# Late shared-FFN pieces inside the last sigmoid, their final add on VectorE as a step of its own, and idle matrix products in attention's last group

## The chip, the core and the metric

The kernel runs on one core of a Trainium2 chip. A core has five engines, each with a queue of its own that it works off in order: TensorE (PE; its weight loads are shown as PEld), VectorE (DVE), ScalarE (ACT), GpSimd (POOL) and SyncE (SP, which here only issues DMAs). Engines wait for one another through semaphores. The metric is the device time of one execution in microseconds (us); of several runs the median counts.

## What is computed

An adaptive-norm transformer block on 8 sequences of 512 rows of 256 values, all in f32: latent attention with 16 heads, then a mixture of 16 experts with an expert-choice router (each expert takes the 512 rows with its highest scores) and a shared FFN for all rows. Cut to what matters:

```python
h = _layernorm(x) * (1 + ca) + sa
x = x + ga * attention(h)                      # causal, 16 heads
h = _layernorm(x) * (1 + cb) + sb
# routed experts
scores = sigmoid(h @ gate_w.T)                 # 4096 x 16
topk_score, topk_ids = top_k(scores.T, 512)    # rows per expert
xin = h[topk_ids]
eo = (silu(xin @ gw.T + gb_e) * (xin @ up_w.T + up_b)) @ down_w.T + down_b
out = zeros_like(h).at[topk_ids].add(eo * topk_score)
# shared FFN, all rows
shared = (silu(h @ sh_gate_w.T) * (h @ sh_up_w.T)) @ sh_down_w.T
x = x + gb * (out + shared)
```

## The kernel before

**Attention.** It runs in 32 steps, `steps[n]`, of four heads each; step n belongs to sequence b = n // 4 and group g = n % 4. In the loop at L781 step n does three things side by side: the maxima of the next step (`scores` L569 on PE, `maxima` L575 on DVE), its own exponentials (`scores_t` L598 on PE, `exps` L609 on ACT, a mask on POOL at L613), and the last step's sums over the values (`context` L628 on PE). `fold` (L590, four transposes, then a product on DVE) opens a step, and eight slots follow. Between them, `fill(k)` runs the pieces that `plan(n)` (L662) has put into slot k: norms, projections, the residual of the sequence before. A piece with a cost is moved to a later slot by `laid_out` when PE has no room; a piece with cost 0.0 stays in its slot. In step 31, the last, there is no next step: no `scores` and no `maxima`.

**Shared FFN.** `Shared(b, early)` (L264) does one sequence. Its 24 units are, for each of four blocks f: two gate products and two up products of 512 columns (L276), with Silu on ACT and the product `mid` on DVE (L312); then eight down units of two products of 256 columns (L321). After four down units `put` (L334) multiplies the two finished row tiles by `gb` on DVE (L336), adds x on POOL (L338) and writes the rows to `out` on SP (L339). Sequences 0 and 1 are "early": `plan` takes their units into attention's steps, twice `SHARE[b][g]` at a time, but always whole groups. Sequences 2 to 7, 144 units, go to the queue `late` (L814) and are taken in pairs by `work()` (L816) as filler for PE wherever the rest of the program leaves it idle.

What DVE has to do after a late unit is not issued at once: it is put on the list `later`, and `flush()` (L260) issues all of it, last in first out. `flush()` is called when the next up unit, the next down unit of a new tile or a new sequence begins, and once per bit of the search (L892).

**From attention to the experts.** After step 31 come the `tail` (L823: the last sequence's residual, norm, transposes and router scores, with a pair of units behind each piece), `sigmoid` for the last two sequences (L840; a generator in four parts, about 16 DVE instructions on 128 x 128 values, then two DMAs of the scores), and a transposition of all scores (L872). Then a binary search over 30 bits finds each expert's threshold (L887): per bit DVE counts (L884), PE sums over the sequences (`cnt`, L891), DVE forms `drop` (L894) and `cand` (L896), and one pair of late units goes to PE. Places are then numbered (`gt`, `eq`, `run`, L903 to L943; `pplace` L928), one-hot tables (L962) and index products (L984) give the row numbers `idx` (L995), and four indirect DMAs on POOL gather the first expert's rows (L1002). What is left in `late` runs behind that (L1154), and then the rows are transposed into `xT` (L1014, L1015) and the expert loop begins.

The order is written out by hand: each engine does its instructions in the order in which the program issues them.

## Time and profile before

| what | value |
|---|---|
| median of 3 runs | 1443.43 us (1439.97 to 1443.79) |
| the profiled execution, its own time | 1438.41 us |
| its span, first to last instruction | 1436.7 us |
| PE busy | 1379.9 us, 96% of the span |
| DVE busy | 906.9 us, 63% |
| POOL busy | 561.7 us, 39% |
| ACT busy | 475.9 us, 33% |
| mean granted TensorE clock | 0.970 |
| POOL's adds of x to the shared rows (L338) | 16 of 1398 ns on average |
| DVE's products with gb (L336) | 16 of 688 ns |

The page gives busy time by engine and, for 40 equal slices of the span (35.9 us each), the busy share in tenths; PEclk is the TensorE clock that was granted, in tenths of full speed. A timeline row has start, length, engine, line, operation, names and shapes, how many instructions were merged (x), and in brackets how long the engine stood idle before it and what ended the wait. An f32 product appears as two PE records. A line of the view by stage has a window, its length, and for each engine the busy us and the number of instructions. The chain of work that ended last could be followed back only through the last DMA (2 us), so it says nothing about the middle of the program.

## The change

Four edits, in the same file:

1. `SHARE` for the last sequence becomes (2, 2, 2, 0). Before, step 28 took four units of sequence 1, step 29 eight; now steps 28, 29 and 30 take four each, so that the second group of four down units moves from step 29 to step 30, with its `put`.
2. `put` becomes a generator of two parts: the multiply; then the add of x and the write to `out`. For late sequences the add runs on VectorE instead of GpSimd. The two parts are two entries of `later`, which becomes a queue, first in first out. `flush(n=2)` issues at most two entries; in the search it is `flush(1)`, one entry per bit.
3. The loop over the last sigmoid's four parts calls `work()` after each part. Eight late units thereby run between the parts instead of behind the first gather, and all late units between move forward by eight places. In the order of instructions the sigmoid's first part is followed on VectorE by a multiply and an add of a `put`, the third part by another such pair, and on SP two writes to `out` and one load of `gb` are ahead of the writes of the scores.
4. In step 31 each of the slots 1 to 8 ends with a product of `ident` and 256 columns of `causal`, whose result nobody reads. It goes to one of the three PSUM banks `s`, which the maxima use in the other steps.

```diff
-SHARE = [(0, 0, 0, 0), *[(0, 1, 1, 1)] * 6, (2, 3, 3, 4)]
+SHARE = [(0, 0, 0, 0), *[(0, 1, 1, 1)] * 6, (2, 2, 2, 0)]
...
-    later = []
-
-    def flush():
-        while later:
-            later.pop()()
+    later = deque()
+
+    def flush(n=2):
+        for _ in range(min(n, len(later))):
+            later.popleft()()
...
             if ii == 1 and h == 1:
+                put = self.put(self.py, i2)
                 if self.early:
-                    self.put(self.py, i2)
+                    next(put)
+                    next(put)
                 else:
-                    later.append(lambda py=self.py: self.put(py, i2))
+                    later.append(lambda: next(put))
+                    later.append(lambda: next(put))
 
         def put(self, py, i2):
             ysb = fp.tile([P, 2, D], F32, name="ysb", tag="ysb", bufs=2)
             nc.vector.tensor_tensor(ysb, py, self.gb.unsqueeze(1).to_broadcast([P, 2, D]), ALU.mult)
+            yield
             n = self.b * TT + 2 * i2
-            nc.gpsimd.tensor_tensor(ysb, ysb, x_all[:, n : n + 2, :], ALU.add)
+            eng = nc.gpsimd if self.early else nc.vector
+            eng.tensor_tensor(ysb, ysb, x_all[:, n : n + 2, :], ALU.add)
             nc.sync.dma_start(out_v[:, n : n + 2, :], ysb)
+            yield
...
+    def keep_warm():
+        n = T // 2
+        nc.tensor.matmul(bank_s("warm")[:, 0:n], lhsT=ident, rhs=causal[:, T - n : T], start=True, stop=True)
...
+        if n + 1 == len(steps):
+            for k in range(1, SLOTS):
+                add(k, 0.0, keep_warm)
...
     for _ in sigmoid(B - 2, 2):
-        pass
+        work()
     flush()
...
-            flush()
+            flush(1)
```

## What was predicted

> **What bounds the kernel now.** I read the slices of the page first, then busy time by stage, then the order of instructions in the stages that the change touches.

> ```profile
> PE   8999999999999999997989999999999999999996
> PEclk8899999999999999798999999999999999999998
> ```

> TensorE is busy nearly everywhere; the holes and the lowered clock lie in slices 17 to 22, between the last attention group and the first expert. That is where all the edits are. The experts behind it (773 us to the end) have PE full at clock 1.0 and are not touched: what is won before them comes off the end. The same stretch cut at the clock's own edges (columns: window, length, then busy us and count of PE, PEld, DVE, ACT, POOL, then granted clock, DMA share, GB/s):

> ```profile
> 582.70:589.50 6.80, 6.72 (x36) 4.40 (x40) 2.96 (x14) 2.75 (x7) 1.31 (x3) 0.50 0.00 0
> 596.35:610.00 13.65, 12.94 (x64) 7.50 (x65) 0.23 (x1) 3.62 (x12) 7.64 (x14) 0.50 0.16 44
> 654.97:660.16 5.19, 0.01 (x2) 0.03 (x1) 4.78 (x14) 0.00 (x0) 0.51 (x1) 0.77 0.30 103
> 660.16:668.03 7.87, 6.36 (x18) 5.07 (x19) 2.97 (x11) 0.59 (x1) 1.26 (x1) 0.50 0.63 187
> 668.03:731.03 63.00, 57.84 (x205) 33.09 (x204) 43.44 (x126) 5.97 (x10) 6.31 (x5) 1.00 0.32 116
> 731.03:753.40 22.37, 20.60 (x101) 12.47 (x99) 18.95 (x31) 1.79 (x3) 4.59 (x2) 1.00 0.05 17
> 753.40:771.70 18.30, 17.45 (x62) 10.53 (x58) 4.39 (x8) 1.79 (x3) 5.36 (x5) 1.00 0.31 90
> ```

> See: two stretches at half clock around attention's last group; PE empty for 5.19 us under the sigmoid (DVE 4.78 busy), then half clock for 7.9 us; 5.2 us of holes in the search; PE full of shared pieces in the last row, after the first gather is issued. Two bits of the search, the first with a `mid` product between count and drop, the second with a `put`:

> ```profile
> 682.69 0.28 PE L891 MATMUL cnt<-part,same 128*128 128x1 f32 x2
> 682.96 0.69 DVE L312 TENSOR_TENSOR mid<-pu,sg 128x512 f32<-128x512 f32 x1 [0.76 <-PE pu L276]
> 684.75 0.38 PE L891 MATMUL cnt<-part,same 128*128 128x1 f32 x2
> ...
> 690.92 0.28 PE L891 MATMUL cnt<-part,same 128*128 128x1 f32 x2
> 691.17 0.69 DVE L336 TENSOR_TENSOR ysb<-py,gb 128x512 f32<-128x512 f32 x1 [0.75 <-issue]
> 691.95 1.26 POOL L338 TENSOR_TENSOR ysb<-ysb,x_all 128x512 f32<-128x512 f32 x1 [20.38 <-DVE drop L894]
> 691.96 1.26 DVE L896 SCALAR_TENSOR_TENSOR cand<-drop,cand 128x1 int32<-128x1 int32 x1
> 694.07 0.38 PE L891 MATMUL cnt<-part,same 128*128 128x1 f32 x2 [1.04 <-DVE mask L884]
> ```

> A bit with a mid takes 2.06 us and PE does not wait. In the bit with a put, POOL's add starts 10 ns ahead of the tiny `cand` step, which then lasts 1.26 us (0.16 elsewhere), and PE waits 1.04.

> **The change, part by part.** Times are against the profiled execution: 1438.41 us, of which 1436.7 are span. That execution is 5.0 us below the median of the three timed runs (1443.43), so the saving is taken off the median.

> *Early pieces (SHARE).* Walking the plan, step 29 keeps one group of four down units, and the other goes to step 30; nothing is left over or dropped. A group is 8 products; 16 of them (32 records) took 7.07 us at 763.78, so 3.5 us of PE. Step 29 lasted 19.4 us (fold to fold, 550.8 to 570.1); step 16, which has the full-size PE work that step 29 will have, lasted 17.3: −2.2. Step 30 lasted 16.2 and its load becomes that of steps 14, 22, 26 (17.5, 17.5, 17.8): +1.4. The put that comes along (DVE 0.69, POOL 1.26, an out write on SP) ends at the fold, where DVE is free and waits 2.40 us for pmx; POOL's next piece is 4 us off. Its write stands on SP before `ga`, first read at 607. Net −0.8. Besides, full-size products now lie in step 30's last slots, before 582.7.

> *Idle products.* Eight, ident with 256 columns, one per slot of step 31: nearest row L321, 0.44 us each, 3.5 in all. They are ahead of the next `st_ps` pair on PE's queue. PE waits there for ACT by 0.39 and 0.57 in two of the first four slots, so about 0.6 of the first four is seen, and the others lie in slots that are counted below. What they buy is the clock. [...] in the window before 596.35 no PE gap exceeded 0.57 us, yet the clock fell. [...] In the 3.41 us windows of this trace, I summed columns streamed, weighted by rows times columns of the array in use. From 60 us to the last expert the clock fell after windows of 0.13 to 0.38 and stayed up after those above 0.4 (and two of 0.36 and 0.37). The one at 592.9 has 0.31, the next two 0.17 and 0.19. One idle product adds 0.43/3.41 = 0.13, about two fall in each window: 0.5. The down group adds 0.25 to 0.5 to the window at 579.3 (0.25). So both half-clock stretches should go:
> - 586.3 to 590.0 (fold, `po`): first `st_ps` 1.6 earlier.
> - slots 4 to 7, 596.6 to 604.5, 7.9 us: at full clock with the idle products about 5.5 (pz 0.93 for 1.89, the pairs 0.43 and 0.21 us): −2.4.
> - `po` of the last group: 4.4 at half clock, 2.2 at full: −2.2; first shared product −0.5.
> - visible idle products +0.6.
> Sum −6.1. Bounds: if the clock does not rise, +3; if all are hidden, −7.

> *Pieces between the sigmoid's parts.* Eight late units, in four pairs: two pairs of down (1.97 each) and a gate and an up pair (1.96 each), 7.9 us, fill the hole of 5.2. The DVE chain grows: two puts of 0.69 multiply and 0.69 add go between its parts, some 2.5 us with the overlap of neighbours (0.60 from start to start). Scores ready about 662.5 instead of 660.0, PE done with the up pair at 662.8, the first count at 664.2 instead of 661.95: +2.3. ACT's Silu is 0.6 in its idle time. On SP, two out writes and a `gb` load (0.4 each) pass ahead of score rows and weights; the weights landed by about 690, used at 773. The cold stretch 660.2 to 668.0 goes: the first three bits took 9.7 us where three take 6.2: −3.5 (this includes one put stall of 1.0). Should the 2.3 us of thin PE work around the transposes of the scores fall into one clock window, 1.7 come back.

> *Add on DVE, one piece per bit.* In the search, four more puts of before cost 1.04 to 1.09 each: −4.2. Now the multiply runs between count and drop, as a mid does (no slack left there: 682.69 to 684.75 is just PE's period). The add is put out by the next down or gate, so it stands between `cand` and the next count. Nearest row: back-to-back DVE products, 0.60 apart. Four times +0.6 = +2.4; the bit behind has nothing to flush and cannot give it back. Bounds 0 to 0.69 each. Who waits is count, then PE's `cnt`, then PE's filler. The adds on DVE work beside no POOL work in the search.

> *Behind the search.* All positions move on by eight units. DVE from the last counts to idx: inserted are two puts (1.2, and 0.5 beyond the wait for `pplace`) and a mid (0.6), 2.3; gone are a mid and two multiplies, 1.8, and the stretch of `at_j` and `num` beside POOL (three pieces of 0.72 to 0.77 us, 0.32 on average elsewhere), 1.25. From `pplace` PE has six pairs of 1.72 us and becomes last: idx about 0.7 earlier. Then PE's remaining list:

> ```profile
> 754.95 1.24 POOL L1002 DMA_INDIRECT rows<-rows_d,idx  x1 [2.77 <-DVE mid L312]
> 759.01 0.95 POOL L1002 DMA_INDIRECT rows<-rows_d,idx  x1 [0.30 <-issue]
> 763.78 7.07 PE L321 MATMUL py<-shd,mid 128*128 128x256 f32 x32
> 771.74 1.06 PE L1014 MATMUL pxt<-ident,rows 128*128 128x128 f32 x8 [0.89 <-issue]
> ```

> Ten units behind the gather's issue instead of eighteen; from pi on, PE has a gate pair, an up pair and the 7.07 us of down: 10.5 us. The last gather lands about 3.7 us after 759.0, 9.3 after pi. So the transposes start some 7.7 us earlier counted from the last counts, with 1.7 us of cover left: the gather is late next. Half a microsecond less is waited for POOL's add before xT.

> **Sum.** −0.8 −6.1 +2.3 −3.5 −4.2 +2.4 −7.7 = −17.6; with the smaller end at xT **−18**. The profiled execution would be 1420, the median **1425**.

> **Rivals.**
> 1. All three work: 1425, own range 1420 to 1431, chance 0.66.
> 2. The clock stays low in the last group (for it: [...] that my weighting is fitted; against it: 0.31 to 0.5 crosses the bound by far). The eight products then cost about 0.85 each, half of it seen, and the 6.1 become +3: 1434. Chance 0.13.
> 3. The gather is no longer covered, by 1 to 4 us, or a clock window is lost at the search's start: for it the cover of only 1.7 us; against it DVE and POOL are emptier there. 1428. Chance 0.14.
> 4. The change moves the hole only (DVE's chain from scores to idx being the true bound, so that the eight units were free where they stood). Against it: PE full in the last row above. Within 0.3%, 1443. Chance 0.04.
> 5. Slower: eight units less behind the gather, and PE stands until it lands. It costs landing minus 10.5 us after pi; to outweigh the 18 the gather must land 28.5 us after pi, three times the 9.3 of the trace. Past that, say at 35, 1449. Nothing in the page supports it. Chance 0.03.

> **The numbers.** Rivals 1 to 3 lie between 1420 and 1435; medians of one kernel differ by some microseconds (the three runs spread over 3.8), hence 1414 to 1436. A change of 0.3%, 4.3 us, is what can be told from none. Faster 0.93 (1 to 3), same 0.04, slower 0.03.

> **What would show it.** Clock 1.0 from 560 to 600 us and through the sigmoid; PE holes there under 2 us; no `cand` step over 0.2 us in the search; PE waits of about 0.6, not 1.04, in four bits; six pairs between pplace and pi; transposes of the first expert directly after the last multiply. The prediction is wrong if the clock row shows 0.5 in the last group, or if PE waits for a gather.

## The result, and the profile after

| | before | after |
|---|---|---|
| median of 4 runs on the same chip | 1441.7 us (1438.53 to 1443.79) | 1420.07 us (1419.21 to 1428.17) |
| ratio | | 0.9864, 95% interval 0.9822 to 0.9906 |
| profiled execution, its span | 1438.41, 1436.7 | 1419.94, 1417.8 |
| mean granted TensorE clock | 0.970 | 0.980 |

The changed kernel is faster, by 21.6 us (1.4%) in the medians and by 18.5 in the profiled executions; the interval of the ratio ends below 1. The slices of its page, busy share and clock of TensorE:

```profile
PE   8999999999999999999999999999999999999996
PEclk8899999999999999999999999999999999999998
```

The dent in slices 17 to 22 is gone from both rows. Line numbers have moved with the edits: `cnt` is L904 now, `cand` L909, the count L897, the two parts of `put` L339 and L343, the gather L1015, the transposes of the gathered rows L1027. The same stretch cut by stage, in the view shown before (window, length, busy us and count of PE, PEld, DVE, ACT, POOL, then granted clock, DMA share, GB/s). The stages are: the last group from its first `st_ps` to the first shared product behind it; from the scores to the first count; from the count of `gt`, the first one behind the search, to the gather's issue; from there to the transposes.

```profile
588.05:604.17 16.12, 16.12 (x120) 8.74 (x116) 0.91 (x3) 6.64 (x17) 9.17 (x17) 1.00 0.09 17
647.92:658.62 10.70, 9.30 (x36) 6.21 (x35) 9.26 (x23) 1.18 (x2) 2.13 (x3) 1.00 0.34 108
...
721.38:744.53 23.15, 21.87 (x104) 13.45 (x103) 19.87 (x36) 1.79 (x3) 0.00 (x1) 1.00 0.09 29
744.53:754.40 9.87, 9.04 (x37) 6.70 (x37) 2.83 (x5) 0.60 (x1) 4.08 (x4) 1.00 0.49 138
```

The clock is 1.00 in every row. TensorE fills the last group without a hole; under the sigmoid it works 9.30 of 10.70 us; and behind the gather's issue there are 9.87 us left where there were 16.8 (754.95 to 771.74 in the trace of before). A bit of the search with a `put`, in the timeline of the changed kernel:

```profile
675.75 0.28 PE L904 MATMUL cnt<-part,same 128*128 128x1 f32 x2
...
675.95 0.69 DVE L339 TENSOR_TENSOR ysb<-py,gb 128x512 f32<-128x512 f32 x1 [0.69 <-PE py L321]
...
676.82 0.68 DVE L343 TENSOR_TENSOR ysb<-ysb,x_all 128x512 f32<-128x512 f32 x1
...
678.23 0.38 PE L904 MATMUL cnt<-part,same 128*128 128x1 f32 x2 [0.36 <-DVE mask L897]
```

The add now lies on DVE ahead of the next count (L897, in the last row's bracket), and PE waits 0.36 us for that count instead of 1.04. And the end of the stretch:

```profile
744.53 1.24 POOL L1015 DMA_INDIRECT rows<-rows_d,idx  x1 [94.32 <-DVE mid L312]
...
746.50 7.07 PE L321 MATMUL py<-shd,mid 128*128 128x256 f32 x32
...
748.57 0.94 POOL L1015 DMA_INDIRECT rows<-rows_d,idx  x1 [0.30 <-issue]
...
754.40 1.06 PE L1027 MATMUL pxt<-ident,rows 128*128 128x128 f32 x8 [0.83 <-issue]
```

The transposes follow directly on the last down products and on the last multiply of the shared FFN; nothing waits for the gather, whose last rows landed at 752.4, 2.0 us ahead of the transposes.

Where the time came from, stage by stage (us, start to start, from the two traces; "predicted" is the term on record; the search runs from the first count on DVE to the last `cnt` on PE):

| stage | before | after | difference | predicted |
|---|---|---|---|---|
| step 28, fold to fold | 19.54 | 19.54 | 0 | 0 |
| step 29 | 19.38 | 16.52 | −2.86 | −2.2 |
| step 30 | 16.17 | 17.21 | +1.04 | +1.4 |
| fold 31 to its first `st_ps` | 3.71 | 2.17 | −1.54 | −1.6 |
| slots 0 to 3 | 6.57 | 7.61 | +1.04 | +0.6 |
| slots 4 to 7 | 7.92 | 6.22 | −1.70 | −2.4 |
| `po`, to the first shared product | 4.42 | 2.29 | −2.13 | −2.2 |
| to the scores | 44.26 | 43.75 | −0.51 | −0.5 |
| scores to the first count | 8.75 | 10.70 | +1.95 | +2.3 |
| first count to the last | 68.41 | 62.09 | −6.32 | −5.3 |
| last count to `xT` | 42.67 | 34.43 | −8.24 | −8.1 |
| `xT` to the first expert's Silu | 6.07 | 4.38 | −1.69 | none |
| experts, to the end | 657.60 | 658.32 | +0.72 | 0 |
| sum from fold 28 on | 905.47 | 885.23 | −20.24 | −18 |

In the row for before, slots 3 and 4 are parted at slot 4's second product (596.59), which waits for ACT; its first had started at 595.16. Parted at the first product, as in the row for after, the two rows are 5.14 and 9.35 before, 7.61 and 6.22 after. Their sum is the same either way, 14.49 and 13.83; only the sum should be read as a gain.

What lies ahead of fold 28 is the same program in both kernels, yet its length is not the same: 531.2 us before and 532.6 after, and 529.7 to 538.4 over all profiled executions of this study. It goes with the time at half clock in that stretch: 41.0 us in the five executions of up to 531.2, 58.0 in the two longest. So in the experiments stages are compared, which without a change of clock repeat to 0.02 us, and sums from fold 28 on; the medians carry that scatter of some microseconds.

## The experiments

The theory: TensorE sets the end nearly everywhere from step 29 to the first expert, so the change gains by (a) keeping the clock up through the last group, with the moved group and the idle products, (b) filling the hole under the sigmoid with work that would otherwise stand behind the gather, and (c) taking POOL's add away from beside `cand`. The rivals are with each run. Stages below are measured against the changed kernel, of which each kernel is a variant.

| us against the changed kernel | e1 | e2 | e3 | e4 | e5 | e6 | e7 | e8 |
|---|---|---|---|---|---|---|---|---|
| fold 28 to fold 31 | 0 | +1.8 | 0 | 0 | 0 | 0 | 0 | 0 |
| fold 31 to the shared product | +2.8 | +1.3 | 0 | 0 | +1.0 | 0 | 0 | 0 |
| to the scores | +0.6 | 0 | 0 | 0 | 0 | 0 | 0 | 0 |
| scores to the first count | 0 | 0 | −2.0 | +0.5 | 0 | −0.9 | +6.0 | 0 |
| the search | +1.7 | 0 | +2.8 | +5.7 | 0 | +0.4 | +0.4 | +1.3 |
| last count to `xT` | 0 | 0 | +7.7 | +0.7 | 0 | +7.7 | −0.1 | 0 |
| first expert's Silu | 0 | 0 | 0 | 0 | 0 | 0 | +1.4 | 0 |
| sum, fold 28 to the end | +4.4 | +3.2 | +8.3 | +6.9 | +0.6 | +6.4 | +8.0 | +0.6 |
| median of the runs, us | 1422.2 | 1428.35 | 1426.43 | 1424.74 | 1422.44 | 1428.74 | 1428.4 | 1418.66 |
| ratio to before | 0.9888 | 0.9916 | 0.9901 | 0.9899 | 0.9880 | 0.9911 | 0.9909 | 0.9846 |
| 95% interval | 0.9847 to 0.9929 | 0.9884 to 0.9948 | 0.9869 to 0.9934 | 0.9866 to 0.9932 | 0.9849 to 0.9911 | 0.9881 to 0.9941 | 0.9876 to 0.9942 | 0.9818 to 0.9874 |

The sum also holds the experts, which differed by −0.9 to +0.4 us for no reason that the stages show. Each variant keeps most of the gain over before, and each interval overlaps that of the changed kernel; what an edit is worth is read in its stage.

**e1: no idle products.**

```diff
-        if n + 1 == len(steps):
-            for k in range(1, SLOTS):
-                add(k, 0.0, keep_warm)
```

> All of the change but the eight idle products of step 31. Theory (the products keep the TensorE clock up): the clock falls to half in the last group again, so against the changed kernel slots 0 to 3 are 1.0 us shorter, slots 4 to 7 are 1.7 longer, po 2.1 longer, the first shared product 0.5 longer: +3.3 us, about 1423. Rival (products only cost time, the clock would stay up by itself [...]): -1.0 us, about 1419, no window at half clock.

The last slots in the timeline of this run, PE alone:

```profile
596.34 0.79 PE L604 MATMUL st_ps<-q,k 32*128 32x128 f32 x2 [0.47 <-ACT p L615]
597.05 1.89 PE L405 MATMUL pz<-wgate,h2T 128*128 128x16 f32 x8
...
599.60 4.50 PE L634 MATMUL po<-p,v 128*32 128x512 f32 x32
```

and in that of the changed kernel:

```profile
599.41 0.70 PE L665 MATMUL warm<-causal,ident 128*128 128x256 f32 x2
599.94 0.96 PE L405 MATMUL pz<-wgate,h2T 128*128 128x16 f32 x8
...
601.25 0.70 PE L665 MATMUL warm<-causal,ident 128*128 128x256 f32 x2
601.88 2.36 PE L634 MATMUL po<-p,v 128*32 128x512 f32 x32
```

Without the products the same eight `pz` records take 1.89 us instead of 0.96 and `po` 4.50 instead of 2.36: half clock, from 591.6 to 605.2. Slots 0 to 3 take 6.56 us (1.05 shorter), slots 4 to 7 7.92 (+1.70, both parted as in the row for before), `po` 4.43 (+2.14), then +0.56: **+3.35**, against +3.3 expected. The rival, that the clock stays up by itself, falls. The +1.7 in the search is another half-clock window, at 659.8, of which more below.

**e2: `SHARE` as before.**

```diff
-SHARE = [(0, 0, 0, 0), *[(0, 1, 1, 1)] * 6, (2, 2, 2, 0)]
+SHARE = [(0, 0, 0, 0), *[(0, 1, 1, 1)] * 6, (2, 3, 3, 4)]
```

> All of the change but SHARE, which is (2, 3, 3, 4) again for sequence 7. Theory (fewer units in step 29 let the clock stay up before the last group): step 29 is 2.9 us longer, step 30 is 1.0 shorter, and the first st_ps of the last group comes 1.5 later after its fold because the clock falls near 582 again: +3.4 us, about 1423. Rival (units are only moved from one place to another, the clock does not depend on them): step 29 and 30 differ by 1.9 in all and the clock in the last group is full: +1.9 us or less, about 1421.

The start of step 31 in this run, and then in the changed kernel, PE alone:

```profile
590.56 1.06 PE L596 MATMUL pmx<-ident,mx 128*128 128x128 f32 x4
591.55 2.58 PE L634 MATMUL po<-p,v 128*32 128x512 f32 x16
...
585.88 0.60 PE L596 MATMUL pmx<-ident,mx 128*128 128x128 f32 x4
586.41 1.71 PE L634 MATMUL po<-p,v 128*32 128x512 f32 x16
```

Step 29 is 2.86 us longer, step 30 1.02 shorter, and the first `st_ps` comes 1.33 later, with the clock at half from 586.5 to 593.3: **+3.2**, against +3.4 expected. So the move is worth 1.8 us as a move (in before, PE is busy for all 19.38 us of step 29, and for 14.86 of the 16.17 us of step 30) and 1.3 through the clock.

**e3: nothing in the sigmoid.**

```diff
     for _ in sigmoid(B - 2, 2):
-        work()
+        pass
```

> Nothing runs on TensorE between the four parts of the last sigmoid; the eight late units are then behind the search, where they were before the change; all else as changed. Theory (work in the sigmoid is TensorE work taken out of the stretch behind the search): from the scores to the first count -1.9 us, the first bits of the search +2.4 at a low clock, behind the search +7.7: +8.2 us, about 1428. Rival (the hole is only moved): within 1 us of the changed kernel.

By stage, for the stretch of the sigmoid and the first bits of this run:

```profile
650.60:660.14 9.54, 2.86 (x13) 1.94 (x12) 8.28 (x21) 0.58 (x1) 2.13 (x3) 0.72 0.28 82
660.14:668.00 7.86, 7.86 (x25) 6.17 (x26) 3.41 (x12) 0.00 (x0) 0.00 (x0) 0.69 0.95 331
```

PE stands for most of the first row, and the first bits begin at half clock. The stages give −1.96, +2.80 and +7.66 us, against −1.9, +2.4 and +7.7 expected: **+8.5** (+8.3 with the experts, which were 0.2 shorter in this run). The hole was not moved but filled, and the work was taken out of the stretch behind the search.

**e4: the add on POOL.**

```diff
-            eng = nc.gpsimd if self.early else nc.vector
+            eng = nc.gpsimd
```

> The add of x stays on GpSimd for the late sequences too, still as a step of its own in two pieces. Theory (the GpSimd add stalls the next candidate on VectorE): in each of four bits the candidate is 1.1 us longer and the 0.36 us of the add on VectorE is saved, so the search is 4 x (1.04 - 0.36) = 2.7 us longer, and 0.5 more behind it: about 1423. Rival (the gain came from splitting put in two): no difference, 1420, the candidate stays at 0.16 us.

A bit with a `put` in its timeline:

```profile
678.66 1.26 POOL L343 TENSOR_TENSOR ysb<-ysb,x_all 128x512 f32<-128x512 f32 x1 [23.69 <-DVE drop L907]
678.68 1.26 DVE L909 SCALAR_TENSOR_TENSOR cand<-drop,cand 128x1 int32<-128x1 int32 x1
...
680.78 0.38 PE L904 MATMUL cnt<-part,same 128*128 128x1 f32 x2 [1.04 <-DVE mask L897]
```

The stall is back as it was before the change: `cand` at 1.26 us and PE waiting 1.04, four times. Splitting `put` had no part in that. The 5.7 us by which the search is longer hold 2.7 of these waits (4 × 0.68); the other 3.0 I put down to a half-clock window of 6.8 us at 657.6, which the changed kernel's profile does not have. Run e8 has such a window at the same place, and against it the search here is 4.41 us longer, 4 × 1.10. That is the whole price of the POOL add in four bits. Behind the search it costs another 0.7 (0.5 expected), most of it because `xT` waits for it: `xT` comes 1.28 us behind the first transpose, as in before, and 0.73 in the changed kernel.

**e5: idle products on a quarter of the rows.**

```diff
-        nc.tensor.matmul(bank_s("warm")[:, 0:n], lhsT=ident, rhs=causal[:, T - n : T], start=True, stop=True)
+        nc.tensor.matmul(bank_s("warm")[:, 0:n], lhsT=ident[0:HS, :], rhs=causal[0:HS, T - n : T], start=True, stop=True)
```

> The eight idle products of step 31 read 32 partitions instead of 128: same moving columns, so the same time on TensorE, a quarter of the array's rows. Theory (the clock goes by how much of the array works): they weigh a quarter, the clock falls in the last group as without them, and their time is still there: slots 4 to 7 +1.7, po +2.1, first shared product +0.5 against the changed kernel, about 1424. Rival (any product, or the absence of gaps, keeps the clock): 1420, no window at half clock.

```profile
598.89 1.89 PE L405 MATMUL pz<-wgate,h2T 128*128 128x16 f32 x8
...
601.87 3.69 PE L634 MATMUL po<-p,v 128*32 128x512 f32 x32
```

Both rows of this run's timeline are at half clock: it fell at 597.8, for 6.8 us, though in the 3.4 us before that PE's longest gap was 0.24 us, and the products' own times add up to 88% of it (those that run side by side counted each; 51% has at least one). So in this run the same eight products with a quarter of the rows did not hold the clock. But the cost was missed: +1.0 us in this group instead of +4.3. Half-clock time was half that of e1 (6.8 us for 13.7), and the products took little time of their own, because here they ran beside those of the attention, which use 32 rows as well: at full clock an idle product starts at 596.59 beside a pair of `st_ps` of 596.57, and ends with it. The clock fell as the theory said; the cost was smaller.

**e6: idle products in the sigmoid instead of work.**

```diff
     for _ in sigmoid(B - 2, 2):
-        work()
+        [keep_warm() for _ in range(4)]
```

> Between the parts of the last sigmoid there are four idle products of 256 columns each time instead of the late units, which are then behind the search. Theory (the gain there has two parts, useful work and a clock that stays up for the first bits): the clock part is kept, some 3 us, the useful work is not: 1425, against 1428 with nothing in the sigmoid. Rival (the clock in the sigmoid is worth nothing): as with nothing in the sigmoid.

The first bits, over the same length as in the second row of e3:

```profile
663.49:671.35 7.86, 6.67 (x29) 4.92 (x30) 5.23 (x17) 0.60 (x1) 0.00 (x0) 1.00 0.96 340
```

No half-clock window there: the search is 2.38 us shorter than in e3, the first count 1.09 later. So the clock in the first bits is worth 2.4 us and the idle filler takes back 1.1, a net 1.3 where 3 was expected. Of the 8.5 us of e3, then, 2.4 is the clock. The rest is work: 7.7 behind the search, less the 2.0 by which it puts off the first count, and 0.4 in the search, where e3 and e6 have five `put`s and the changed kernel four.

**e7: sixteen units in the sigmoid.**

```diff
     for _ in sigmoid(B - 2, 2):
-        work()
+        work(2)
```

> Sixteen late units between the parts of the last sigmoid instead of eight. Theory (only some 2 us of TensorE work is left over the gather, so more units moved ahead of the search uncover it): the first count 6.2 us later, the copy of the first gathered rows only about 2 us earlier after it, perhaps a window at half clock while TensorE waits: +4 to +6, about 1425, with TensorE idle before the first product on gathered rows. Rival (all is bound by TensorE, so it does not matter where the units run): 1420 within 1.

```profile
760.21 0.30 PE L1027 MATMUL pxt<-ident,rows 128*128 128x128 f32 x1 [1.51 <-DVE ysb L343]
...
760.38 0.94 POOL L1015 DMA_INDIRECT rows<-rows_d,idx  x1 [0.30 <-issue]
...
763.48 0.48 PE L1027 MATMUL pxt<-ident,rows 128*128 128x128 f32 x1 [1.48 <-DMA rows<-rows_d,idx]
...
765.19 1.33 PE L1027 MATMUL pxt<-ident,rows 128*128 128x128 f32 x5 [1.24 <-DMA rows<-rows_d,idx]
```

PE has run out of work and waits for the gather, transpose by transpose, at half clock from 762.4. The first count is 5.98 us later, and nothing comes back: `xT` is as far behind the last count as in the changed kernel (−0.06, where about −2 was expected), because the index arithmetic ended 0.9 later too and the last rows landed 4.8 us after their issue. With the half-clock window the stages give **+7.7** (+8.0 with the experts) instead of +4 to +6. Sixteen units are too many; numbers between eight and sixteen were not tried.

**e8: the add one bit later.** The second piece of a `put` is marked True. While the search runs, the units no longer flush a piece so marked (`settle` takes the place of their `flush()`); it goes out with the next bit's `flush(1)`, behind that bit's `cnt`.

```diff
-                    later.append(lambda: next(put))
-                    later.append(lambda: next(put))
+                    later.append((lambda: next(put), False))
+                    later.append((lambda: next(put), True))
...
+    def settle():
+        while later and not (searching[0] and later[0][1]):
+            later.popleft()[0]()
```

> The add of x stays on VectorE but is issued one bit later, ahead of the next bit's cast while TensorE counts, instead of right behind the candidate. Theory (behind the candidate it delays the next count by 0.36 us in each of four bits): -1.4 us, about 1418.5. Rival (TensorE has work queued, the delay is hidden): 1420.

```profile
678.88 0.69 DVE L349 TENSOR_TENSOR ysb<-ysb,x_all 128x512 f32<-128x512 f32 x1
...
679.01 0.38 PE L911 MATMUL cnt<-part,same 128*128 128x1 f32 x2
...
679.48 0.15 DVE L914 TENSOR_SCALAR drop<-cnt 128x1 int32<-128x1 f32 x1
```

The add lies beside `cnt`, which starts with no wait. In this profile a half-clock window at 657.2 hides the gain (the search is 1.3 us longer than the changed kernel's). The run e9 below, without such a window, shows it.

**The start of the search.** In e1, e4 and e8 the clock fell there, in the changed kernel's profile, e2 and e5 it didn't, with the same code between the scores and the first count but for e4's add. The last three runs look at this; they ran on one chip.

> The changed kernel once more, on the chip of the next two runs, to have its times beside theirs: 1420 to 1424. If a half-clock window opens at the start of the search it is because a throttle window there weighs 0.34 or less (it weighed 0.43 in the profile of the changed kernel; 0.25, 0.32 and 0.34 with the same code in three others, where the clock fell).

The changed kernel once more: 1418.66 us (1417.21 to 1421.73), ratio 0.9861 (0.9837 to 0.9886). This time the clock did fall, at 656.8, after a window of 0.28, and the search took 1.6 us longer than in its first profile.

> The add one bit later, as before, and three idle products in the hole of TensorE between the last unit of the sigmoid and the first count: one before the four transposes, two after them. Theory (the clock falls at the start of the search where a window weighs 0.34 or less, by the luck of where the windows lie; three products of 0.63 us add up to 0.55 to such a window and fit in the hole): no window at half clock before the first bits in any position, the first count is not later, the search takes 61.3 - 1.4 = 59.9 us: about 1418 and a narrower spread. Rival (the products delay the transposes or the first count): +0.5 to +2 from the scores to the first count, 1420.

> The changed kernel with the same three idle products, the add where the change put it. Theory: the search takes 61.3 us with no window at half clock in front of it, 1 to 2 us better than the changed kernel in the median, because only about half of its runs have the clock fall there. Rival: the products delay the first count, +0.5 to +2.

```diff
     for _ in sigmoid(B - 2, 2):
         work()
+    keep_warm()
...
+        keep_warm()
+        keep_warm()
         nc.scalar.copy(s2, pt)
```

PE in the timeline of e9:

```profile
656.48 0.59 PE L671 MATMUL warm<-causal,ident 128*128 128x256 f32 x2
657.33 0.63 PE L892 MATMUL ps<-ident,scores 128*128 128x128 f32 x4 [0.26 <-DVE scores L444]
657.79 1.03 PE L671 MATMUL warm<-causal,ident 128*128 128x256 f32 x4
659.47 0.38 PE L914 MATMUL cnt<-part,same 128*128 128x1 f32 x2 [0.64 <-DVE mask L906]
```

The products fit: transposes and first count come no later (10.69 us from the scores, as before), no window is at half clock in either run, and the lightest window there weighs 0.65 (e9) and 0.64 (e10). The search takes 62.11 us in e10 and 60.21 in e9 (61.3 and 59.9 expected), so the delayed add is worth 1.9 us there (1.4 expected; the other 0.5 is not explained). Fold 28 to the first expert: 226.9 us for the changed kernel in its luckier profile, 228.5 in the other, 226.9 for e10, **225.0 for e9**. In the medians this is lost in the scatter of what lies ahead: e9 1418.31 us (1414.26 to 1421.21), ratio 0.9849 (0.9822 to 0.9875); e10 1420.5 us, ratio 0.9873 (0.9848 to 0.9898). The intervals overlap that of the changed kernel, and the 1 to 2 us that e10 was to gain in the median were not seen. e9 beats the change by stages, not measurably by time.

## Why the prediction was right

Of the profiled execution the forecast was 1420 us, and it took 1419.9; the median was forecast at 1425 and came to 1420.07. That the first pair agrees so closely is luck: from fold 28 on the saving was 20.2 us for 18, and ahead of fold 28, in code that the change leaves alone, this execution lost 1.4. The median forecast was the saving of 18 us taken off 1443.43, the median of three runs of before; with the later run of before added that median is 1441.7. All forecast mechanisms are there, with errors of 0.1 to 1.7 us that partly cancel:

- **Early pieces.** −1.82 instead of −0.8. Mis-sized in step 29: it was compared with step 16 (17.3 us) and came out at 16.52. e2 takes the move back alone.
- **Idle products.** −4.84 instead of −6.1. The clock terms held (first `st_ps`, `po`, first shared product to within 0.1). What was too small was the products' own price: the eight slots took 13.83 us where the forecast gives 12.7, and ACT, not PE, now waits in them (0.45 to 1.34 us in front of the first exponential of each slot behind slot 0), so each product delays the next pair of `st_ps`. How that splits between slots 0 to 3 and 4 to 7 depends on where they are parted. The clock was also held by less than the forecast says: it put the windows at about 0.5, and by my estimate (last section) the lightest in the group weighed 0.38, and 0.38 to 0.40 in the nine other profiles with all eight products. All ten kept the clock, but elsewhere in the program windows of 0.36 (249.2 in after) and 0.38 (770.4 in before) lost it.
- **Gaps against window sums.** In before, PE had no gap over 0.57 us in the window ahead of 596.35, yet the clock fell; the forecast went by the window sums. e1 and e5 show the same: the clock fell behind windows in which PE's longest gap was no more than 0.57 us (e1, before 591.68) and 0.24 us (e5).
- **Sigmoid.** The first count +1.95 later for +2.3. The window around the transposes of the scores weighed 0.43 in the first profile, and the clock stayed; that "1.7 come back" if it fell was put down as a possibility, and changed_again shows it (+1.6).
- **Search.** −6.32 for −5.3. Nearly the whole difference is the add between `cand` and the count: 0.36 us four times for 0.6. The add starts 0.08 after `cand` does; from `cand` to the count it is 0.68 us (676.74 to 677.42) where it is 0.19 in the next bit, so the count is 0.49 later. Of that PE sees 0.36: the forecast had allowed it no slack.
- **Behind the search.** −8.24 for −8.1 (−7.7 and the smaller end at `xT`). e3 shows 7.66 of it from the eight units alone. The cover of 1.7 us left was 2.0 (rows landed at 752.4, transposes at 754.40), and in e7, with eight units more taken away, PE waits for the gather.
- **Not in the sum.** The forecast has the experts at clock 1.0 from 773 us on. In truth the trace of before has a half-clock window from 773.8 to 777.2, and the 1.69 us that it cost are gone. It followed a window of 0.38 in which PE waited before the transposes and, with `xT` behind POOL's add, after them. None of the later kernels had it except e7, which waits there for the gather; the lightest window there weighed 0.52 to 0.73 in the others. This gain was not foreseen. The experts' +0.72 is not explained.

Rival 2 (clock stays low in the last group) fell by the change's own profile; of rival 3 the gather was not uncovered at eight units and was at sixteen, while the lost window at the search's start came in changed_again, at 1.6 us; rivals 4 and 5 fell with e3 and with the gather landing in time. The new order of `later` (first in, first out) and the limit of one entry per bit were not varied alone.

## What to carry to other kernels

In this kernel filler was worth most where it took useful work from a later stretch that TensorE bounds: the sigmoid's filler took 7.7 us from there and put off the first count by 2.0; the clock that it kept up gave another 2.4. It has a limit that must be worked out beforehand, here the work that covers a gather: with eight units more, in e7, PE waited 1.48 and 1.24 us for its rows. A small step of the serial search (`cand`, 128x1) lasted 1.26 us instead of 0.16 in all five bits of before, and in four of e4, in which it ran beside a 128x512 add on POOL. What is put on its own engine instead belongs into the time in which that engine waits (behind `cnt`, 1.9 us better in e9 than in e10), not in front of the next count. When changes of 1 to 3 us are judged in a kernel whose half-clock windows differ from run to run (the changed kernel's search: none in its first profile, one in its second, 1.6 us), compare stages of the traces, and look for the windows first.

## What the runs showed of the hardware

**The clock in the traces.** In the traces of before and after, the stretches at half clock last 3.41, 6.83, 10.24, 13.65 or 20.48 us (only the one that the trace's end cuts off differs), which are 1, 2, 3, 4 and 6 times 3.41. The clock's first record begins 5.8 us behind the first instruction in before and 6.9 in after, and the edges lie at multiples of 3.41 from there. For each window of 3.41 us on that grid I summed the time in which products streamed their columns: 0.21 us for a record of 256 columns at full clock, since such records follow one another by 0.216 us in the median in after; twice that at half clock, as records of 512 columns follow by 0.43 and 0.85. The weighted sum takes each product's time by rows times columns of the array in use over 128 × 128; this weighting is an estimate of mine from those spacings and the records' shapes. Products that run side by side count each in the sum, so a column says in what share of the window at least one streamed. Some windows, all from the part of the program that the change touches:

| window (run, start) | sum | share with at least one | weighted sum | clock in the next window |
|---|---|---|---|---|
| e5, 594.4 | 0.88 | 0.51 | 0.24 | half |
| e1, 588.1 | 0.83 | 0.54 | 0.30 | half |
| before, 592.9 | 0.87 | 0.57 | 0.31 | half |
| e8, 653.8 | 0.34 | 0.34 | 0.34 | half |
| e2, 661.6 | 0.37 | 0.37 | 0.37 | full |
| before, 770.4 | 0.38 | 0.38 | 0.38 | half |
| after, 597.4 | 0.66 | 0.48 | 0.38 | full |
| changed_again, 595.4 | 0.71 | 0.51 | 0.39 | full |
| after, 655.4 | 0.43 | 0.43 | 0.43 | full |

**From run to run.** The same code at the start of the search kept the clock in some profiles (windows of 0.37 to 0.46: the changed kernel, e2, e5) and lost it in others (0.25 to 0.34: e1, e8, changed_again), for 1.6 to 3 us. The windows lay differently there: one began at 655.4 in the changed kernel's first profile, and in changed_again the clock fell at 656.8.
